# Zero rows under two matrix products, and a margin on the landings in a planned schedule

## The chip, the cores and the metric

One core of a Trainium2 chip runs the whole program. The time is the device time of one execution in microseconds, the median of the runs shown. The profile is of one execution of its own, so sums over its rows are set against that execution's time.

## The reference

The input x is 32 images of 96 channels and 56 x 56 pixels, float32. Two residual layers follow each other; each begins with a group normalisation over groups of three channels.

```python
x = x + _L0_conv_ref(_gn(x), ...)
x = x + _L1_conv_ref(_gn(x), ...)
```

Layer 0 is an inverted bottleneck with quantised weights and activations: a 1x1 convolution from 96 to 576 channels, batch norm, clipping to 4 bits; a 3x3 depthwise convolution, batch norm, clipping to 4 bits; a 1x1 convolution back to 96 channels, batch norm.

Layer 1 splits the 96 channels into three parts of 32. One goes through a gated 3x3 convolution, one through a fractional Fourier transform, a gated 1x1 mix, the inverse transform and an absolute value, and one through a real FFT, a gated 1x1 mix and the inverse FFT. The gates are small networks on channel means. The three parts are joined and go through a last 3x3 convolution from 96 to 96 channels.

## The kernel before

Each image is 96 partitions by 3136 floats and is worked on alone; images overlap only through the order of the instructions. Three buffers hold x.

Layer 0. `split` (line 702) normalises a quarter of the image (the four parities of row and column) into v on VectorE, rounds it on ScalarE to `hi`[...], and takes the rest `lo` on GpSimd. `expand` (712) multiplies both by w1 into a pair of PSUM banks: 2 halves by hi and lo, 392 columns each, with a contraction over 96 rows; this is tile pe. ScalarE's Relu (line 662) writes 8-bit levels q1s, VectorE masks them (666). Then the levels go to DRAM (sd, line 738) and come back in another layout (d, 746) for the depthwise products pd (756), which are column-tiled: 128 rows by 64 columns, two side by side. Their levels q2s go to DRAM (gd, 777) and come back (q, 780) for the projection pp (786), which adds into x (796). There are 5 blocks of 128 channels, the last of 64, so pe, pd and pp share two PSUM pairs in a fixed rotation.

Layer 1. `norm` (859) writes a part of F, which goes to DRAM (xd, 868) and back in another layout (xh, 875). Small products pf, pu, pi, pv carry out the transform forward and back. The result pq goes to DRAM (pd, line 1024, another tensor than the PSUM tile of that name) and comes back as F in four transfers (1029 and 1033, two each). `mix_f` (1041) multiplies F, 98 rows, by the gates into pz (line 1047), squares, adds, takes the root and copies into cat on GpSimd. `spatial` (1122, tile ps) and `mix_t` (1103, tile px) write the other parts of cat. `winograd` (1144) turns cat on VectorE into V, T and U, and `final` (1174) multiplies six slices V by the transformed weights wc into pc (line 1179): float32, 96 rows by 96 columns, 392 columns moving, three taps each. The results are added to x, and `store` writes x out.

The order has two makers. `arrange` (381) runs through three streams of steps, head (statistics and split), body (the rest of layer 0) and rest (layer 1), and picks the next step by how far each stream is through its work plus a lead in images: -0.8, 0.0 and 1.0 (line 1298). This fixes the order in which buffers and PSUM banks are handed round. Then the class `Order` plans every instruction: `model` (208) gives each a duration, and each DMA a time to landing (line 236); `pack` (277) is a list scheduler that puts them on the engines by rank[...]. `schedule` (339) tries 3 x 8 rankings and keeps the shortest plan. `hold` fixes each engine's order from it. A plan's times bind nothing on the chip; only its order does, and every engine takes its instructions in that order.

All DMAs of the steady state are issued by SyncE, in one order.

Of the kernel before, what the change touches and what calls it, by code (L numbers as in the profile page):

```python
# [52 lines left out]
F32 = mybir.dt.float32  # L53
# [25 lines left out]
BN_EPS = 1e-5  # L79
WINDOW, CHANGE = 3.4133, 0.09  # L80
TURNS, NEAR = 8, (2.0, 4.0, 8.0)
SLACK = 0.3


# [58 lines left out]
class Order:  # L143
# [64 lines left out]
    def model(self):  # L208
# [3 lines left out]
        for i, e, access in zip(self.ins, self.eng, self.access):  # L212
# [6 lines left out]
            if i.opcode == "DMACopy":  # L219
                took = 0.47 if e == "SP" else 0.4  # L220
                for a in (outs[0], ins[0]):
                    run = size = _bytes(a.dtype)
                    dims, n = list(a.ap), 1.0
                    if self.tiles.get(a.tensor.name, "dram") != "dram":
                        n = dims.pop(0)[1]
                        move = max(move, _count(a) * size / 7000.0 * min(n / 16.0, 1.0))
                    for _, c in dims:
                        n *= c
                    for step, c in reversed(dims):
                        if step * size == run or c == 1:  # L230
                            run *= c
                        else:
                            break
                    run = min(run, n * size / 16)
                    move = max(move, math.ceil(n * size / run / 16) * (0.011 + run / 21e3))
                lag = 1.6 + move + (0.3 if ins[0].tensor.name.startswith(("in_x", "sd", "gd")) else 0.0)
            elif e == "PE":
                cols, weights, rows = _count(ins[0]), _count(ins[1]), ins[0].ap[0][1]
                full = all(str(a.dtype) == "dt.float32" for a in ins)
                beside = weights in (G, 64) and cols >= HN  # L240
                if i.is_transpose:
                    took = max(cols / 1175.0, 0.055)
                    work = cols / 1200.0
                elif full:
                    took = 2 * max(cols / 1175.0, min(weights * 0.85e-3, 1.0), 0.05)
                    work = cols / 600.0
                else:
                    took = max(cols / (2180.0 if "float32r" in str(ins[1].dtype) else 2350.0), 0.05)
                    work = cols / 2400.0
                if beside and not i.is_transpose:  # L250
                    took, work = took * weights / 128.0, work * weights / 128.0
                kind = (0 if rows <= 32 else 1 if rows <= 64 else 2), weights if beside else 0
                work *= rows / 128.0
            elif e == "Activation":
                out = _count(outs[0])
                bias = sum(_count(a) == 1 for a in ins) > 1
                took = 0.1 + bias * 0.1 + out / 960.0 + (0.08 if out > 700 and psum[0] else 0.13 if out < 8 else 0.0)
            elif e == "DVE":
                port = n > 8 and not any(psum)
                if port and i.opcode == "TensorScalarPtr" and len(wide) == 1:  # L260
                    took = 0.15 + n / 1920.0 + (0.12 if n >= 700 else 0.0)
                else:
                    port = port and len(wide) > 1
                    took = (0.14 if n > 8 else 0.16) + n / 960.0 + (0.06 if any(psum) and "ScalarPtr" in i.opcode else 0.0)
            elif e == "Pool":
                port = True
                took = 0.1 + n * (2.25 if len(wide) > 1 else 1.1) / 1000.0 if n > 8 else 0.5
            else:
                took = 0.1
# [178 lines left out]
def block_kernel(ctx: ExitStack, tc: tile.TileContext, out: bass.AP, a: dict):  # L448
# [38 lines left out]
    with tc.tile_pool(name="prep", bufs=1) as pp:  # L487
# [22 lines left out]
                nc.vector.tensor_copy(dst, w, saturate=False)  # L510


        w1 = cp.tile([C, 128 * NB], F32R, tag="w1r", name="w1r")
        nc.vector.memset(w1[:, HID:].bitcast(F32), 0.0)
        quantise(load_tmp("w1"), C, "1", w1[:, :HID])
        w2 = load_tmp("w2")
        quantise(w2, 128, "2")
        nc.vector.tensor_tensor(w2, w2, load_tmp("mask2"), ALU.mult)
# [50 lines left out]


        raw = load_tmp("wc")
        wc = cp.tile([C, 6, 3 * C], F32, tag="wcw", name="wcw")
        tap = lambda k: raw[:, 3 * C * k : 3 * C * (k + 1)]
        sm = pp.tile([C, 3 * C], F32, tag="wsum", name="wsum")
        nc.vector.tensor_scalar(wc[:, 0, :], tap(0), 1.0 / 4, None, ALU.mult)
# [50 lines left out]
        q2.append(t)  # L626
    s0 = cp.tile([128, QS], F32, tag="s0", name="s0")
    nc.gpsimd.memset(s0, 0.0)
    cat = cp.tile([C, H + 2, W + 2], F32, tag="cat", name="cat")
    nc.gpsimd.memset(cat, 0.0)  # L630

    def group_stats(s, stats, name):

# [39 lines left out]
    def layer0(i):  # L673
# [16 lines left out]
        def norm():  # L690
            mean, rstd = s["mean"], s["rstd"]
            stats2[i] = p2.tile([C, 8, 6], F32, tag="bn2", name=f"bn2{i}")

            ab = p2.tile([C, 2], F32, tag="ab", name=f"ab{i}")
            nc.vector.tensor_scalar(ab[:, 0:1], rstd, 1.0, None, ALU.add)
            nc.vector.tensor_scalar(ab[:, 1:2], mean, rstd, None, ALU.mult)
            nc.vector.tensor_tensor(ab[:, 1:2], B3, ab[:, 1:2], ALU.subtract)
            s["ab"] = ab
            s["hi"] = p1.tile([C, 4, 2 * HN], F32R, tag="hi", name=f"hi{i}")
            s["lo"] = p1.tile([C, 4, 2 * HN], F32R, tag="lo", name=f"lo{i}")  # L700

        def split(u):
            v = p1.tile([C, 2 * HN], F32, tag="v", name=f"v{i}_{u}")
            nc.vector.tensor_scalar(  # L704
                v.rearrange("p (h w) -> p h w", w=HH), parity(u), s["mean"], s["rstd"], ALU.subtract, ALU.mult
            )
            nc.scalar.copy(s["hi"][:, u, :], v)  # L707
            nc.gpsimd.tensor_tensor(s["lo"][:, u, :], v, s["hi"][:, u, :].bitcast(F32), ALU.subtract)  # L708
            if u == 3:
                nc.gpsimd.tensor_scalar(xts[i], xts[i], s["ab"][:, 0:1], s["ab"][:, 1:2], ALU.mult, ALU.add)  # L710

        def expand(b, u):
            k = blk(b)
            ps = pair(f"pe{i}_{b}_{u}")
            for half in range(2):
                for n, part in enumerate((s["hi"], s["lo"])):
                    nc.tensor.matmul(  # L717
                        ps[:, half, :HN],
                        w1[:, 128 * b : 128 * (b + 1)],
# [134 lines left out]
    def layer1(i):  # L854
# [289 lines left out]
        def winograd(half, part):  # L1144
# [1 line left out]
            pitch = W + 2  # L1146
            n = 7 * pitch
            if part == 0:
                s["V", half] = p1.tile([C, 6, n], F32, tag=("torus", "F")[half], name=f"V{i}_{half}")
                s["T"] = p1.tile([C, 4, n], F32, tag="cs", name=f"T{i}_{half}")  # L1150
                s["U"] = p1.tile([C, 7, 2 * pitch], F32, tag="Z", name=f"U{i}_{half}")
            V, T, U = s["V", half], s["T"], s["U"]

            d = lambda j, m: view(catf, pitch * (28 * half + j), [[4 * pitch, 7], [1, m * pitch]])
# [19 lines left out]
        def final(half, k):  # L1174
# [3 lines left out]
            for dx in range(3):  # L1178
                nc.tensor.matmul(  # L1179
                    ps[:C, :HN],  # L1180
                    wc[:, k, C * dx : C * (dx + 1)],
                    V[:, :, dx : dx + W],
                    start=(dx == 0),
                    stop=(dx == 2),
                )
# [109 lines left out]
        rest += layer1(i)  # L1295
    for x in head[:13]:
        x.after.pop((-1, "e", NB - 1, 3), None)
    arrange([head, body, rest], loose, {"pair": 2, "bank": 4}, [-0.8, 0.0, 1.0], B)
    Order(nc.cur_bb.bb.instructions, tiles).hold(tc)


# [218 lines left out]
```

## Time and profile before

| what | value |
|---|---|
| median of three runs | 3350.51 us (3349.19 to 3354.25) |
| the profiled execution | 3364.8 us |
| its span, first to last instruction | 3363.0 us |
| mean granted TensorE clock | 0.949 |
| VectorE / ScalarE / GpSimd busy | 69% / 62% / 17% |
| DMA moved | 469.92 MB, 140 GB/s |
| waits of ScalarE for pd | 454.5 us |
| pe on hi and on lo | 1280 each, 416 and 344 ns |

In the rows of the profile a product is named by the PSUM tile it writes, then what it reads, then rows * columns of the array. A float32 product is two instructions, so pc has 2304 for 1152 products. The number in square brackets in a timeline is idle time of that engine just before, with what ended it.

### The profile page before, as it was taken

The numbers are of one execution on the slowest core, as the hardware profiler recorded it, in microseconds if no ns is written. First come the engines' busy times: TensorE is split into PE (matmuls) and PEld (weight loads), VectorE is DVE, ScalarE is ACT, GpSimd is POOL, SyncE is SP. The second block draws the span as 40 slices with busy tenths as digits, with TensorE's granted clock in tenths as the row PEclk, the third lists the DMA queues.
The fourth block names the chain that finished last, engine by engine and source line by source line (L and its number), as shares of the span: only waits on it lengthen the run. The fifth ranks groups of instructions, "written<-read, shape, count | busy, mean of one in ns | idle before, by whom it ended". The sixth has DMA issues, their size and how long they took to land. (4 is left out here: it accounts for less than half of the span.)

```text
span 3363.0 us, 47042 instructions
## 1 busy us (share of the span) xinstructions
PE 2961.3 (88%) x17024; PEld 1824.1 (54%) x17024; DVE 2331.5 (69%) x4497; ACT 2085.9 (62%) x2792; POOL 585.2 (17%) x657
## 2 busy tenths in 40 slices
PE   3789998889998889999899999898998898999987
PEld 2455565455565555555455565455565455565544
DVE  5357677677777676777677777676777676777755
ACT  3566665576666566656566666566666576666543
POOL 3122101222101222111222011222111222101100
PEclk9898999999999999999999999999999999999987
DMA  4545564455655455654455655455655455655432
GB/s 125 150 118 143 147 166 133 116 144 144 167 159 141 117 145 137 168 141 134 124 146 151 173 146 149 121 146 138 168 157 142 116 145 143 166 162 148 115 89 51
DMA packets 436800, 469.92 MB, mean 140 GB/s; under 512 B 203174, under 2 KB 351640, under 8 KB 435544
## 3 DMA queue, kind: packets, MB, share of 16 engines
q1 hardware_dynamic: 432384, 464.18, 51.6%
q10 hardware_dynamic: 4184, 2.74, 0.3%
q8 instruction: 135, 2.21, 0.3%
q14 instruction: 97, 0.79, 0.1%
HBM read 266.85 MB, written 199.97 MB: 139 GB/s over the span
## 5 line engine op out<-in xcount | busy, mean ns | idle before, releaser
L662 ACT ACTIVATE q2s<-pd,o,s 128x784 uint8<-128x784 f32 x576 | 558.3, 1002 | 473.9 <-PE pd L756 454.5
L1179 PE MATMUL pc<-V,wcw 96*96 96x392 f32 x2304 | 834.9, 502 | 18.1 <-DVE V L1164 18.1
L662 ACT ACTIVATE q1s<-pe,o,s 128x784 uint8<-128x784 f32 (+1 forms) x640 | 624.1, 1004 | 219.7 <-PE pe L717 213.5
L717 PE MATMUL pe<-hi,w1r 96*128 96x392 f32 x1280 | 532.7, 416 | 68.0 <-ACT q1s L662 32.1
L1179 PEld LDWEIGHTS pc<-V,wcw 96*96 96x96 f32 x2304 | 366.9, 164 | 338.9 <-issue 319.7
L756 PE MATMUL pd<-d,dw 128*64 128x392 fp8e4 x4608 | 471.1, 345 | 85.1 <-DMA d<-sd 78.2
L717 PE MATMUL pe<-lo,w1r 96*128 96x392 f32 x1280 | 440.6, 344 | 3.2 <-POOL lo L708 3.2
L756 PEld LDWEIGHTS <-dw 128*64 128x64 bf16 x4608 | 243.3, 113 | 297.8 <-DMA d<-sd 104.8
L717 PEld LDWEIGHTS pe<-hi,w1r 96*128 96x128 f32 x1280 | 242.9, 190 | 181.4 <-ACT q1s L662 88.2
L708 POOL TENSOR_TENSOR lo<-v,hi 96x784 fp32r<-96x784 f32 x128 | 243.4, 1901 | 287.9 <-ACT hi L707 274.6
L1047 PE MATMUL pz<-F,g 98*32 98x392 f32 x1024 | 178.0, 700 | 129.3 <-DMA F<-pd 79.3
L786 PE MATMUL pp<-q,w3q 128*96 128x392 fp8e4 x1280 | 269.5, 359 | 12.1 <-DMA q<-gd 9.5
L717 PEld LDWEIGHTS pe<-lo,w1r 96*128 96x128 f32 x1280 | 244.2, 191 | 27.5 <-POOL lo L708 4.2
L786 PEld LDWEIGHTS <-w3q 128*96 128x96 fp8e4 x1280 | 167.2, 135 | 154.4 <-issue 70.6
L666 DVE TENSOR_SCALAR q2s<-q2s 128x392 uint32<-128x392 uint32 x288 | 119.4, 421 | 182.9 <-ACT q2s L662 180.0
L796 DVE SCALAR_TENSOR_TENSOR x<-pp,s,x 96x392 f32<-96x392 f32 x256 | 146.1, 617 | 103.9 <-PE pp L786 103.7
L654 POOL TENSOR_TENSOR stb<-veb,mhalf 96x1 f32<-96x1 f32 x32 | 17.9, 561 | 1143.8 <-DVE veb L653 1143.8
L1060 POOL COPY cat<-sq 32x392 f32<-32x392 f32 x256 | 157.8, 616 | 295.7 <-ACT sq L1056 286.1
L666 DVE TENSOR_SCALAR q1s<-q1s 128x436 uint32<-128x436 uint32 (+1 forms) x320 | 122.6, 389 | 120.5 <-ACT q1s L662 99.6
L704 DVE TENSOR_SCALAR v<-x,sta 96x784 f32<-96x784 f32 x128 | 87.0, 680 | 161.1 <-POOL lo L708 139.5
L1126 PE MATMUL ps<-s,g 128*128 128x392 f32 x512 | 193.6, 503 | 0.0
L1140 ACT ACTIVATE cat<-ps,b 32x392 f32<-32x392 f32 x256 | 158.8, 620 | 46.2 <-PE ps L1126 42.5
(156 smaller groups left out, 4267.8 us busy)
## 6 DMA issues: line engine op xcount, KB each, us to landing
d<-sd SPq DMA_DIRECT2D x288, 435.5 KB
gd<-q2s SPq DMA_DIRECT2D x288, 196.0 KB
sd<-q1s SPq DMA_DIRECT2D x256, 218.0 KB
q<-gd SPq DMA_DIRECT2D x128, 392.0 KB
x<-in_x_dram SPq DMA_DIRECT2D x128, 294.0 KB
out_dram<-x SPq DMA_DIRECT2D x128, 294.0 KB
pd<-pq SPq DMA_DIRECT2D x32, 808.5 KB
F<-pd SPq DMA_DIRECT2D x64, 392.0 KB
```

The lines of the kernel that those rows point to most:

```text
L662: nc.scalar.activation(dst, ps, AF.Relu, bias=offset, scale=scale)
L666: nc.vector.tensor_scalar(w, w, 4, 0x0F0F0F0F, ALU.logical_shift_right, ALU.bitwise_and)
L708: nc.gpsimd.tensor_tensor(s["lo"][:, u, :], v, s["hi"][:, u, :].bitcast(F32), ALU.subtract)
L717: nc.tensor.matmul(ps[:, half, :HN], w1[:, 128 * b : 128 * (b + 1)], part[:, u, HN * half : HN * (half + 1)], start=(n == 0), stop=(n == 1),)
L756: nc.tensor.matmul(ps[64 * t : 64 * (t + 1), half, :HN], dw[n][:, 2 * t + y, :], view(s["d"][b, g][:, t, :], PQ * (14 * half + y), [[PQ, 1 ...
L786: nc.tensor.matmul(ps[:C, half, :HN], w3[:, b * C : (b + 1) * C], q2[b][:, u, HN * half : HN * (half + 1)], start=(b == 0), stop=(b == NB ...
L796: nc.vector.scalar_tensor_tensor(part, src, A3, part, ALU.mult, ALU.add)
L1047: nc.tensor.matmul(ps[G * j : G * (j + 1), :HN], s["g1"][: 3 * G + 2, G * q : G * (q + 1)], s["F"][:, 2 * HN * j + HN * h : 2 * HN * j + H ...
L1060: nc.gpsimd.tensor_copy(cat[G : 2 * G, r : r + 7, 1 : 1 + W], src)
L1126: nc.tensor.matmul(ps[:, :HN], s["g0"][:, 128 * t : 128 * (t + 1)], view(s0, PQ * (14 * half + t // 2) + t % 2, [[PQ, 14], [1, HH]]), star ...
L1140: nc.scalar.activation(dst, src, AF.Identity, bias=b0[2 * G : C], scale=1.0)
L1179: nc.tensor.matmul(ps[:C, :HN], wc[:, k, C * dx : C * (dx + 1)], V[:, :, dx : dx + W], start=(dx == 0), stop=(dx == 2),)
```

## The change

The products pe and pc contract over 128 rows in place of 96; the 32 rows added are zeros. For this w1 becomes a tile of 128 partitions, all set to zero before the weights are written into the first 96. hi and lo become one tile each for the whole kernel, with rows 96 to 127 set to zero once, in place of a new tile for each image. The weights wc lie in a tile wcz of 128 partitions with its last rows zero. cat, V, T and U get 128 partitions; cat's last rows stay zero from its first memset, and VectorE's operations that make V, T and U run over all 128 partitions.

The planner adds MARGIN, 0.8 us, to each DMA's time to landing. The lead of layer 1 in `arrange` goes from 1.0 to 0.95 images.

```diff
+MARGIN = 0.8
...
-                lag = 1.6 + move + (0.3 if ins[0].tensor.name.startswith(("in_x", "sd", "gd")) else 0.0)
+                lag = 1.6 + MARGIN + move + (0.3 if ins[0].tensor.name.startswith(("in_x", "sd", "gd")) else 0.0)
...
-        w1 = cp.tile([C, 128 * NB], F32R, tag="w1r", name="w1r")
-        nc.vector.memset(w1[:, HID:].bitcast(F32), 0.0)
-        quantise(load_tmp("w1"), C, "1", w1[:, :HID])
+        w1 = cp.tile([128, 128 * NB], F32R, tag="w1r", name="w1r")
+        nc.vector.memset(w1.bitcast(F32), 0.0)
+        quantise(load_tmp("w1"), C, "1", w1[:C, :HID])
...
-        wc = cp.tile([C, 6, 3 * C], F32, tag="wcw", name="wcw")
+        wcz = cp.tile([128, 6, 3 * C], F32, tag="wcw", name="wcw")
+        nc.gpsimd.memset(wcz[C:], 0.0)
+        wc = wcz[:C]
...
-    cat = cp.tile([C, H + 2, W + 2], F32, tag="cat", name="cat")
+    cat = cp.tile([128, H + 2, W + 2], F32, tag="cat", name="cat")
     nc.gpsimd.memset(cat, 0.0)
+    hi, lo = (cp.tile([128, 4, 2 * HN], F32R, tag=k, name=k) for k in ("hi", "lo"))
+    for t in (hi, lo):
+        nc.gpsimd.memset(t[C:].bitcast(F32), 0.0)
...
-            s["hi"] = p1.tile([C, 4, 2 * HN], F32R, tag="hi", name=f"hi{i}")
-            s["lo"] = p1.tile([C, 4, 2 * HN], F32R, tag="lo", name=f"lo{i}")
...
-            nc.scalar.copy(s["hi"][:, u, :], v)
-            nc.gpsimd.tensor_tensor(s["lo"][:, u, :], v, s["hi"][:, u, :].bitcast(F32), ALU.subtract)
+            nc.scalar.copy(hi[:C, u, :], v)
+            nc.gpsimd.tensor_tensor(lo[:C, u, :], v, hi[:C, u, :].bitcast(F32), ALU.subtract)
...
-                for n, part in enumerate((s["hi"], s["lo"])):
+                for n, part in enumerate((hi, lo)):
...
-                s["V", half] = p1.tile([C, 6, n], F32, tag=("torus", "F")[half], name=f"V{i}_{half}")
-                s["T"] = p1.tile([C, 4, n], F32, tag="cs", name=f"T{i}_{half}")
-                s["U"] = p1.tile([C, 7, 2 * pitch], F32, tag="Z", name=f"U{i}_{half}")
+                s["V", half] = p1.tile([128, 6, n], F32, tag=("torus", "F")[half], name=f"V{i}_{half}")
+                s["T"] = p1.tile([128, 4, n], F32, tag="cs", name=f"T{i}_{half}")
+                s["U"] = p1.tile([128, 7, 2 * pitch], F32, tag="Z", name=f"U{i}_{half}")
...
-                    wc[:, k, C * dx : C * (dx + 1)],
+                    wcz[:, k, C * dx : C * (dx + 1)],
...
-    arrange([head, body, rest], loose, {"pair": 2, "bank": 4}, [-0.8, 0.0, 1.0], B)
+    arrange([head, body, rest], loose, {"pair": 2, "bank": 4}, [-0.8, 0.0, 0.95], B)
```

## The prediction

> **What bounds the kernel now.** I read the page first (shares, clock row, costliest groups), then the waits, then one period of the steady state: TensorE's and SyncE's timelines and the busy time by stretches. The page says that TensorE is the engine to watch, and that its clock is not full.
>
> ```profile
> span 3363.0 us, 47042 instructions
> PE 2961.3 (88%) x17024; PEld 1824.1 (54%) x17024; DVE 2331.5 (69%) x4497; ACT 2085.9 (62%) x2792; POOL 585.2 (17%) x657
> PEclk9898999999999999999999999999999999999987
> L1179 PE MATMUL pc<-V,wcw 96*96 96x392 f32 x2304 | 834.9, 502 | 18.1 <-DVE V L1164 18.1
> L1047 PE MATMUL pz<-F,g 98*32 98x392 f32 x1024 | 178.0, 700 | 129.3 <-DMA F<-pd 79.3
> ```
>
> The reader is to see two things: 402 us (3363.0 less 2961.3) in which TensorE does nothing, and a granted clock of 0.949 on average. Nearly a third of that idle time, 129.3 us, stands before one small product, pz (line 1047). The timelines of TensorE and SyncE around one such place:
>
> ```profile
> 1010.73 1.55 PE L1110 MATMUL px<-torus,g 128*32 128x392 f32 x16
> 1012.07 0.26 PE L1112 MATMUL px<-pat,bias 128*32 128x56 f32 x2
> 1016.30 4.14 PE L1047 MATMUL pz<-F,g 98*32 98x392 f32 x20 [3.97 <-ACT cat L1120]
> 1020.37 2.81 PE L786 MATMUL pp<-q,w3q 128*96 128x392 fp8e4 x12
> ...
> 1003.40 0.32 SPq L1024 DMA_DIRECT2D pd<-pq  x1
> ...
> 1008.62 1.19 SPq L1029 DMA_DIRECT2D F<-pd  x2
> 1009.86 2.13 SPq L1033 DMA_DIRECT2D F<-pd  x1
> 1012.03 0.53 SPq L777 DMA_DIRECT2D gd<-q2s  x1
> 1012.60 0.78 SPq L1033 DMA_DIRECT2D F<-pd  x1
> ```
>
> The wait is put down to ScalarE's copy of cat, but that copy starts at 1015.73 and frees nothing that pz reads; what pz reads is F, whose fourth transfer is issued only at 1012.60. One image later the same wait (3.81 us before 1116.14) is put down to F<-pd. In TensorE's timeline 28 of the 32 images have this gap before pz, 3.6 to 6.0 us, 123 us in all. A second gap, before pd (line 756) and put down to d<-sd, is there in 9 images: 33 us.
>
> Behind each gap the clock is halved. [...]the columns are busy us of TensorE, weight loads, VectorE, ScalarE, GpSimd (instructions in brackets), the clock, DMA share and GB/s:
>
> ```profile
> 1011.39:1014.81 3.42, 0.94 (x14) 0.37 (x9) 1.00 (x2) 3.33 (x7) 1.84 (x1) 1.00 1.34 160
> 1014.81:1018.22 3.41, 1.92 (x12) 0.69 (x16) 2.33 (x5) 2.01 (x5) 1.85 (x1) 0.50 0.35 93
> 1018.22:1021.63 3.41, 3.41 (x16) 1.28 (x9) 2.04 (x2) 2.76 (x4) 3.17 (x2) 0.50 0.01 3
> 1021.63:1025.04 3.41, 3.41 (x24) 1.67 (x23) 2.41 (x5) 0.53 (x1) 3.26 (x4) 1.00 0.00 0
> ...
> 100.06:103.46 3.40, 1.52 (x16) 0.81 (x16) 0.36 (x1) 2.80 (x4) 0.00 (x0) 1.00 0.80 217
> 103.47:106.87 3.40, 0.00 (x0) 0.00 (x0) 0.86 (x2) 0.96 (x2) 1.83 (x1) 1.00 0.40 61
> ...
> 632.54:635.95 3.41, 1.95 (x9) 1.32 (x8) 1.42 (x4) 3.41 (x5) 1.55 (x3) 1.00 0.24 77
> 635.95:639.36 3.41, 0.38 (x4) 0.23 (x6) 2.97 (x4) 0.08 (x1) 2.24 (x2) 0.50 0.68 192
> ```
>
> In all, 338 us run at half clock, about 100 windows in some 48 episodes (0.051 of the clock lost, times two, times the span).[...] The window from 100.06 holds 16 pd products of 128 rows[...] and the next stays fast. The one from 632.54 holds [...]pe products with 96 rows, and the next is slow.[...]
>
> [...]the 128-row ps (line 1126) takes 503 ns, the 96-row pc 502, both f32 with 392 columns.[...]
>
> **The change, part by part.**
>
> *Zero rows.* pe (lines 717) and pc go from 96 to 128 rows: by the rows above 0 ns an instruction, 4864 of them.[...] Gain 10 us. The pz episodes don't change by this: their windows are filled with pz, which keeps 98 rows, and pp, which has 128.[...]
>
> *VectorE on 128 partitions.* The V, T, U operations do the same number of elements a partition (T 1867 ns for 1624): nothing.
>
> *Memsets at the start.* w1: 640 columns in place of 64 (0.11 us); a 576-column pass takes 1.04 us (line 505), so 1.2 at most, and VectorE idles from 0.9 to 10.2 us. hi and lo: two of 3136, like cat's 3364 in 3.17 us, so 2 x 2.95; wcw's rows 1728, 1.6. GpSimd idles 7.6 us before sta and 9.6 before the first lo, which hides 7.5 us. Nothing; uncovered, 7.5 us once.
>
> *hi and lo kept for good.* An image's first split no longer waits for all readers of the tile before, only for those of its own quarter. In the stretch above the splits of the next image run from 1005 to 1018, while the last pe of this one ended at 984: they wait for x and its statistics, not for the tile. Nothing.
>
> *The margin.* It changes no instruction, only the planner's idea of when data is there, so the order. Two hops lead to pz. The planner prices pd at 0.47 + 1.6 + 7 x (0.011 + 7392/21000) = 4.6 us; in the timeline F's first issue follows pd's by 5.2. It prices F's four at 0.47 + 0.63 + 2 x 2.43 + 2 x 0.09 + 0.97 = 7.1 us; pz starts 7.7 after the first issue. Together it is 1.2 us short, and the margin gives 1.6. SyncE alone explains part: a line-1033 issue takes 2.0 us (median), the planner says 0.47. The other 2.8 of the usual 4.4 us are not a mispriced landing: they are either in the plan or come from elsewhere, and the margin won't fill them. What could fill even the 1.6? pp waits for the last block's q (issued 1016.00), its two open sums hold both PSUM pairs, so pe of the next image can't start; pc waits for pz. Work must be moved here from the pd, pp and ps of the 10 us before, which leaves a smaller gap there. So I take half.
> In full: 28 x 1.6 = 45 us idle[...]. The pd gap: 9 x 1.6 = 14[...]. Sum 80, half is 40 us. Bounds: 0 and 80.
> A margin adds no wait. But consumers are put later: behind a pz put later stand sq, cat, V and pc, and behind pc the store and the load of x three images on.
>
> *Lead 1.0 to 0.95.* Layer 1 is taken 0.05 image, 5 us of the 101 us between one pz and the next 20 times over, earlier against layer 0. It fixes which PSUM bank follows which; its sign I can't read. Zero, with 60 us either way.
>
> Sum: 10 + 40 = 50 us off the profiled execution's 3364.8, so 3315. The median of the runs shown, 3350.5, lies 14.3 below that execution; there it is 3300.
>
> **Rivals.**
>
> *The gap is filled.* Lead and margin together move F's wait under the depthwise products. For it: 1035 to 1085 us TensorE is idle for 0.4 us, so work abounds one stage away. Against it: what blocks here is PSUM and q. Then all of 123 + 63 goes at best, say three quarters, and 10 of padding: 3350 - 150 = 3200.
>
> *The plan already holds the wait.* Then the margin only names it, and padding alone pays: 3340. For it: 2.8 of 4.4 us have no mispriced hop. Against it: the planner ranks by the whole chain and shifts whole groups.
>
> *Longer plan, slower kernel.* x has three buffers: load, statistics, split, layer 0, layer 1 and store of one image make a loop of three periods. Ten DMA hops lie on it (x; sd, d, gd, q of the last block; xd, xh, pd, F; out): 10 x 0.8 / 3 = 2.7 us a period in the plan, 85 us over 32. If half of that becomes real, since consumers that used to start at once now stand behind other work in TensorE's queue, it is 40 us more than before: 3390. For it: x is loaded at 985, right behind the store of 975 to 980. Against it: at most hops data does come later than planned. It decides from where the distance from pz to pz passes 102 us.
>
> **How the numbers follow.** Partly filled, 0.52: 3300, own range 3265 to 3335. Filled, 0.15: 3200. Padding alone, 0.13: 3340, half of it within 0.2% (7 us, about what a measurement of this kernel can tell from no change). Slower, 0.20: 3390, of which 0.01 within. Faster 0.74, same 0.07, slower 0.19. The range, 3200 to 3372, leaves out half of each outer case.
>
> **What would show it.** Right: the gap before pz falls from 4.4 to about 2.8 us or less, half-clock windows from 100 to about 75, clock about 0.96, pe and pc as long as before, hops as long as before. Wrong: pz's gap unchanged in most images (padding alone); gaps of over 3 us before pe, pp or pf that weren't there (longer plan); pe or pc over 1% longer each (rows are not free).

## The result: no change, and where the idle time went

The changed kernel takes 3351.39 us (median of 12 runs, 3339.75 to 3367.20) against 3355.18 for the kernel before in the same session. The ratio of the mean times is 1.0001, with a 95% interval of [0.9984, 1.0018] (the ratio of the two medians is 0.9989). The forecast was 3300. Its profiled execution took 3365.41 us (before 3364.8).

The page of the changed kernel: span, busy time of each engine, granted clock in 40 slices, the row of pc.

```profile
span 3363.6 us, 47169 instructions
PE 2972.1 (88%) x17024; PEld 1832.9 (54%) x17024; DVE 2340.7 (70%) x4497; ACT 2091.1 (62%) x2792; POOL 626.0 (19%) x660
PEclk9889999999999999999999999999999999999997
L1184 PE MATMUL pc<-V,wcw 128*96 128x392 f32 x2304 | 835.7, 499 | 13.0 <-DVE V L1169 13.0
```

TensorE is idle for 391.5 us (3363.6 less 2972.1), it was 401.7. Half-clock time is 319 us, it was 343 (the prediction's 338 is a slip: its own product gives 343), and the mean clock 0.953 instead of 0.949. The zero rows cost no time: pc is 499 ns for 502, pe on lo 349 for 344, and from the start of one pc instruction to the next the median is 329 ns in both. (Lines have shifted by 5 to 7.) So nearly all idle time is still there. It isn't where it was. These are groups by line, first of the kernel before, then of the changed kernel, with the idle time just before each in the last column (pz of the kernel before stands in the prediction):

```profile
L756 PE MATMUL pd<-d,dw 128*64 128x392 fp8e4 x4608 | 471.1, 345 | 85.1 <-DMA d<-sd 78.2 <-ACT q2s L662 5.2 <-ACT q1s L662 1.2
L786 PE MATMUL pp<-q,w3q 128*96 128x392 fp8e4 x1280 | 269.5, 359 | 12.1 <-DMA q<-gd 9.5 <-ACT q2s L662 2.1 <-DVE x L796 0.5
L986 PE MATMUL pu<-u,e2t 112*114 112x456 f32 x128 | 63.9, 604 | 10.7 <-ACT u L977 10.6
...
L761 PE MATMUL pd<-d,dw 128*64 128x392 fp8e4 x4608 | 470.3, 345 | 29.7 <-DMA d<-sd 21.6 <-ACT q1s L669 5.0 <-ACT q2s L669 2.2
L791 PE MATMUL pp<-q,w3q 128*96 128x392 fp8e4 x1280 | 277.5, 375 | 86.2 <-DVE x L801 73.0 <-DMA q<-gd 11.3 <-ACT q2s L669 1.7
L1052 PE MATMUL pz<-F,g 98*32 98x392 f32 x1024 | 134.8, 595 | 78.1 <-DMA F<-pd 59.4 <-DVE cat L1123 13.5 <-DVE v L709 5.1
L991 PE MATMUL pu<-u,e2t 112*114 112x456 f32 x128 | 81.0, 746 | 71.8 <-ACT u L982 71.7
```

Before pz the idle time fell from 129.3 to 78.1 us, before pd from 85.1 to 29.7: 107 us less, where the prediction asked 59 us of the margin (45 and 14, before it halved the sum). But before pp it rose from 12.1 to 86.2 and before pu from 10.7 to 71.8: 135 us more. The margin isn't the only cause of this move. Every edit here, the zero rows too, makes the planner choose another order, and in the run with the zero rows alone (e1 below) pz and pu stand much as they do in the changed kernel:

```profile
L1052 PE MATMUL pz<-F,g 98*32 98x392 f32 x1024 | 143.1, 631 | 76.4 <-DMA F<-pd 75.3 <-DVE cat L1123 0.7 <-issue 0.3
L991 PE MATMUL pu<-u,e2t 112*114 112x456 f32 x128 | 74.9, 672 | 73.3 <-ACT u L982 70.2 <-ACT torus L1093 2.5 <-DVE torus L1091 0.3
```

The prediction had held that the waits before pz don't change by the zero rows. One place in TensorE's timeline of the changed kernel:

```profile
1014.77 1.20 PE L791 MATMUL pp<-q,w3q 128*96 128x392 fp8e4 x6
1018.16 4.63 PE L1052 MATMUL pz<-F,g 98*32 98x392 f32 x32 [2.19 <-DMA F<-pd]
1022.72 2.52 PE L791 MATMUL pp<-q,w3q 128*96 128x392 fp8e4 x14
1026.82 3.35 PE L791 MATMUL pp<-q,w3q 128*96 128x392 fp8e4 x19 [1.58 <-DVE x L801]
```

and VectorE's timeline beside it:

```profile
1021.07 0.68 DVE L709 TENSOR_SCALAR v<-x,sta 96x784 f32<-96x784 f32 x1 [0.86 <-POOL lo L713]
1021.67 0.56 DVE L1060 TENSOR_TENSOR sq<-sq 128x392 f32<-128x392 f32 x1
1024.62 0.95 DVE L709 TENSOR_SCALAR v<-x,sta 96x784 f32<-96x784 f32 x1 [2.40 <-POOL lo L713]
1025.61 2.22 DVE L801 SCALAR_TENSOR_TENSOR x<-pp,s,x 96x392 f32<-96x392 f32 x4
```

Projection products now stand ahead of pz, so its wait is 2.19 us here, where the same place before had 3.97. But pp needs a PSUM bank back, which VectorE's add into x (line 801) gives; that add stands in VectorE's queue behind v (line 709) of the next image, and v waits 2.40 us for GpSimd's lo. A new wait, with the same work behind it.

### The profile page after: what moved, and what is told of

The parts are those of the page before. It is cut to its first block, busy times and chain, and to the rows that moved or that the text cites. A ratio compares the mean times of both kernels' runs of the same rounds, so it can differ in the third digit from the quotient of the medians.

```text
span 3363.6 us, 47169 instructions
## 1 busy us (share of the span) xinstructions
PE 2972.1 (88%) x17024; PEld 1832.9 (54%) x17024; DVE 2340.7 (70%) x4497; ACT 2091.1 (62%) x2792; POOL 626.0 (19%) x660
## 5 line engine op out<-in xcount | busy, mean ns | idle before, releaser
L1184 PE MATMUL pc<-V,wcw 128*96 128x392 f32 x2304 | 835.7, 499 | 13.0 <-DVE V L1169 13.0
L722 PE MATMUL pe<-hi,w1r 128*128 128x392 f32 x1280 | 519.5, 406 | 50.2 <-DVE x L801 21.2
L1184 PEld LDWEIGHTS pc<-V,wcw 128*96 128x96 f32 x2304 | 363.6, 163 | 315.6 <-issue 298.2
L761 PE MATMUL pd<-d,dw 128*64 128x392 fp8e4 x4608 | 470.3, 345 | 29.7 <-DMA d<-sd 21.6
L722 PE MATMUL pe<-lo,w1r 128*128 128x392 f32 x1280 | 444.8, 349 | 3.2 <-POOL lo L713 3.2
L791 PE MATMUL pp<-q,w3q 128*96 128x392 fp8e4 x1280 | 277.5, 375 | 86.2 <-DVE x L801 73.0
L722 PEld LDWEIGHTS pe<-hi,w1r 128*128 128x128 f32 x1280 | 243.8, 191 | 167.3 <-ACT q1s L669 75.6
L722 PEld LDWEIGHTS pe<-lo,w1r 128*128 128x128 f32 x1280 | 245.3, 192 | 22.8 <-POOL lo L713 4.2
L661 POOL TENSOR_TENSOR stb<-veb,mhalf 96x1 f32<-96x1 f32 x32 | 30.3, 947 | 1135.3 <-DVE veb L660 1135.3
L1052 PE MATMUL pz<-F,g 98*32 98x392 f32 x1024 | 134.8, 595 | 78.1 <-DMA F<-pd 59.4
L1145 ACT ACTIVATE cat<-ps,b 32x392 f32<-32x392 f32 x256 | 158.4, 619 | 41.2 <-PE ps L1131 37.2
L1007 PEld LDWEIGHTS pi<-e,cs 114*114 114x114 f32 x1088 | 133.8, 189 | 58.6 <-issue 52.1
L673 DVE TENSOR_SCALAR q2s<-q2s 128x392 uint32<-128x392 uint32 x288 | 103.9, 361 | 87.2 <-ACT q2s L669 87.0
```

What stands on the lines that cost most here:

```text
L673: nc.vector.tensor_scalar(w, w, 4, 0x0F0F0F0F, ALU.logical_shift_right, ALU.bitwise_and)
L722: nc.tensor.matmul(ps[:, half, :HN], w1[:, 128 * b : 128 * (b + 1)], part[:, u, HN * half : HN * (half + 1)], start=(n == 0), stop=(n == 1),)
L761: nc.tensor.matmul(ps[64 * t : 64 * (t + 1), half, :HN], dw[n][:, 2 * t + y, :], view(s["d"][b, g][:, t, :], PQ * (14 * half + y), [[PQ, 1 ...
L791: nc.tensor.matmul(ps[:C, half, :HN], w3[:, b * C : (b + 1) * C], q2[b][:, u, HN * half : HN * (half + 1)], start=(b == 0), stop=(b == NB ...
L1052: nc.tensor.matmul(ps[G * j : G * (j + 1), :HN], s["g1"][: 3 * G + 2, G * q : G * (q + 1)], s["F"][:, 2 * HN * j + HN * h : 2 * HN * j + H ...
L1145: nc.scalar.activation(dst, src, AF.Identity, bias=b0[2 * G : C], scale=1.0)
```

## The experiments

"Period" is the mean distance from the first pz of one image to that of the next, over images 4 to 28, from each run's trace; it was 100.80 us before and is 100.57 after. Ratios are to the kernel before on the same chip, with 95% intervals. Three theories come up: P, that TensorE's gaps are lost time and the margin moves or fills them; L, that the loop of the three x buffers sets the period; and R, the ring, that layer 1 of one image can't begin before that of the image before has ended, so that its whole chain is one period long. A caution for all of them: nearly every edit leads the planner to another order of the instructions, so a run shows its edit together with that order. Only e9 has the order of the kernel that it is set against.

**The parts and their pairs.** e1: zero rows alone. e2: margin alone. e3: lead alone. e5: zero rows and margin. e6: zero rows and lead.

```diff
 e1, from after     -MARGIN = 0.8                +MARGIN = 0.0
                    -[-0.8, 0.0, 0.95]           +[-0.8, 0.0, 1.0]
 e2, from before    -lag = 1.6 + move            +lag = 1.6 + 0.8 + move
 e3, from before    -[-0.8, 0.0, 1.0]            +[-0.8, 0.0, 0.95]
 e5, from after     -[-0.8, 0.0, 0.95]           +[-0.8, 0.0, 1.0]
 e6, from after     -MARGIN = 0.8                +MARGIN = 0.0
```

> Zero rows and the kept hi and lo alone; no margin, lead 1.0. Theory A (waits only move: the stretch where both layers wait has a fixed length, whatever the order): 0.996 to 1.004 of before, with the gap before pz still about 4.4 us in most images. Theory B (the parts have real effects of opposite sign that cancel): padding saves the 10 us that I had priced, 0.995 to 0.998, with fewer half-clock windows before pd.

> The margin of 0.8 us alone; no zero rows, lead 1.0. Theory A: 0.997 to 1.004; the gap before pz falls to about 2 us, and new gaps of the same sum stand before pp, pu or pe. Theory B: clearly off 1, either 0.985 to 0.99 (margin good, lead bad) or 1.01 and more (margin bad, the others good).

> The lead of 0.95 alone; no zero rows, no margin. Theory A: 0.997 to 1.004. Theory B: clearly off 1 by 0.5% or more, with the sign opposite to the margin's.

> The changed kernel with the lead back at 1.0: zero rows and margin. If the margin's loss of 1.3% (seen alone) is its own: 1.008 to 1.012 of before, with the gap before pd in most images as with the margin alone. If it came from one unlucky phase of the two layers that the lead mends: the same, so this can't tell these two apart, but a result at 1.000 would say that the zero rows change the plan enough to undo it.

> The changed kernel with MARGIN 0: zero rows and lead 0.95. If the parts add: 0.9965 x 1.0022 = 0.9987 of before, so that the margin inside the change would cost 0.14%. If the margin helps once the lead is right: 1.003 or more.

| lead | zero rows | no margin | margin |
|---|---|---|---|
| 1.0 | no | 1 | e2: 1.0126 [1.0109, 1.0143] |
| 1.0 | yes | e1: 0.9965 [0.9954, 0.9975] | e5: 1.0098 [1.0079, 1.0117] |
| 0.95 | no | e3: 1.0022 [1.0003, 1.0041] | e9 (below): 1.0026 [1.0010, 1.0041] |
| 0.95 | yes | e6: 0.9990 [0.9978, 1.0003] | the change: 1.0001 [0.9984, 1.0018] |

Down each column the zero rows take 0.25 to 0.35% off. The margin costs 1.3% at lead 1.0; at 0.95 it is 0.1%, within the noise. The lead costs 0.2% without a margin and gains 1.0% with it. So the change is a gain of 0.3% by the zero rows and a loss of about as much by margin and lead together. That the two cancel to 1.0001 is chance. Of the theories A and B in these expectations, A falls with e2. B is right about the zero rows and the margin, but not about the lead, whose sign alone isn't opposite to the margin's. In e5 the time is what was expected, but its idle time stands before pc (162.2 us) and not before pd.

In e2 the margin does to pz what it was to do. Two groups of e2, then two lines of TensorE's timeline:

```profile
L756 PE MATMUL pd<-d,dw 128*64 128x392 fp8e4 x4608 | 488.2, 355 | 156.3 <-DMA d<-sd 139.0 <-ACT q2s L662 13.1 <-ACT u L977 2.1
L1047 PE MATMUL pz<-F,g 98*32 98x392 f32 x1024 | 120.4, 514 | 12.1 <-DMA F<-pd 9.3 <-ACT cat L1120 2.8
```

```profile
1028.28 2.82 PE L756 MATMUL pd<-d,dw 128*64 128x392 fp8e4 x16 [3.99 <-DMA d<-sd]
1032.81 3.58 PE L1179 MATMUL pc<-V,wcw 96*96 96x392 f32 x5 [1.71 <-DVE V L1164]
```

The wait before pz is gone (12.1 us for 129.3). Products pe of the next image fill its place, and with them used up, pd waits for its data some 4 us in 31 places: 156.3 us for 85.1. Here this gap and the next, before pc, are 3 us apart and stand at half clock together (0.50 in each stretch from 1025.90 to 1036.10). TensorE's idle time in all is 423 us, for 402 before, half-clock time 424 us for 343, and the clock 0.938. So the wait was filled, and TensorE was idle for longer.

**Rows, with the order held.** e9 has the instructions of the changed kernel in its order on every engine, with only the rows of pe and pc back at 96; its planner is told that they have 128.

```diff
-                        w1[:, 128 * b : 128 * (b + 1)],
-                        part[:, u, HN * half : HN * (half + 1)],
+                        w1[:C, 128 * b : 128 * (b + 1)],
+                        part[:C, u, HN * half : HN * (half + 1)],
...
-                    wcz[:, k, C * dx : C * (dx + 1)],
-                    V[:, :, dx : dx + W],
+                    wcz[:C, k, C * dx : C * (dx + 1)],
+                    V[:C, :, dx : dx + W],
```

> The changed kernel with pe and pc contracting over 96 rows again; the planner still counts 128 rows for them, so every engine's order is that of the changed kernel. It isolates what the zero rows do on the chip. If rows weigh[...]: slower than the changed kernel by 5 to 20 us, some more windows at half clock, and pe and pc no shorter. If rows don't weigh: the same time and the same number of windows at half clock as the changed kernel.

1.0026 [1.0010, 1.0041], against 1.0001 of the changed kernel. The groups of e9:

```profile
L1187 PE MATMUL pc<-V,wcw 96*96 96x392 f32 x2304 | 842.9, 502 | 12.6 <-DVE V L1172 12.6
L725 PE MATMUL pe<-hi,w1r 96*128 96x392 f32 x1280 | 524.8, 410 | 53.8 <-DVE x L804 25.5 <-ACT hi L715 15.0 <-ACT q1s L672 9.2
```

Its products are as long (pc 502 ns) and its half-clock time is 340 us instead of 319. Over all runs its mean clock is 0.951 (16 runs), that of the changed kernel 0.956 (12 runs). With the same order on every engine, that is what the rows did to the granted clock. In time it is 0.25%, and the two ratios' intervals overlap. The four pairs of the table have one sign, but in three of them the order differs too.

**What sets the period.** e12: the changed kernel with three x tiles for good, so that each quarter of x can be loaded as soon as it is free. e13: the kernel before with two x buffers in place of three (a load then waits for the store two images back). e18: the kernel before with the operation `norm` (line 863) done three times over. e14: e1 with pz over 128 rows, the rows added to F being zeroed by GpSimd for each image.

```diff
 e12 -        xt = xp.tile([C, HW], F32, tag="x", name=f"x{i}")
     +        xt = xbuf[i % 3]
 e13 -tc.tile_pool(name="xp", bufs=3)), "xp", 3, tiles)
     +tc.tile_pool(name="xp", bufs=2)), "xp", 2, tiles)
 e18 +            for _ in range(3):
                      nc.vector.tensor_scalar(s["F"][2 * G : 3 * G], ...)
 e14 -            s["F"] = p1.tile([G * 3 + 2, HW], F32, tag="F", name=f"F{i}")
     +            s["F"] = p1.tile([128, HW], F32, tag="F", name=f"F{i}")
     +            nc.gpsimd.memset(s["F"][3 * G :], 0.0)
     -                        s["g1"][: 3 * G + 2, G * q : G * (q + 1)],
     +                        s["g1"][:, G * q : G * (q + 1)],
```

> The changed kernel with three x tiles kept for good, so that a quarter of x is loaded as soon as that quarter of the image three before is stored, not when all of it is. This shortens the loop load, layer 0, layer 1, store by some 3 to 5 us. If that loop of three periods holds the period (theory L): a third of it a period, 1.0 to 1.7 us, 32 to 54 us in all, 0.984 to 0.990 of the changed kernel. If not: within 0.4% of the changed kernel.

> The kernel before with two buffers of x in place of three. It measures the loop itself: with two, a period is at least half of one image's way from load to store. Theory L (the loop is tight with three): that way is about 300 us even with less company on the engines, so some 150 us a period and 4600 us or more. If the way is much shorter than 300 us when it isn't held up by other work, say 240: 120 us a period, about 3850 us, and the loop isn't what sets 101 us with three.

> The kernel before with layer 1's first operation on F (line 863, 1.9 us on VectorE) done three times over, with the same result; 3.8 us more between one image's last pc and the next image's xd. Theory R (layer 1 is a ring of one period: F takes the place of the V that the last pc of the image before reads, so norm, xd, xh, pf, pu, pi, pv, pd, F, pz, cat, winograd, pc run one after the other and their length is the period): 3.8 us a period, 31 times, 118 us, 1.03 to 1.036 of before. Theory L (the ring of three periods over the x buffers): a third, 1.010 to 1.013. Theory P (TensorE's sum of work and waits): within 0.4%.

> Zero rows alone (no margin, lead 1.0), and pz too: F gets 128 rows, its last 32 set to zero by GpSimd for each image before the two single rows land.[...] If rows weigh: 15 to 25 windows at half clock fewer than with zero rows under pe and pc alone; under theory R only what stands in the ring counts, pz itself, 1 to 2 us a period at best: 0.985 to 0.997 of before.

L has no support. e12 is slower, 1.0187 [1.0163, 1.0211], which neither reading of it had. e13 takes 4182 us with a period of 128.2 us, between its two readings. With two buffers an image goes through in two periods, 256 us, less than the 302 that three periods give now; so the way of an image can be shorter than the three buffers allow.

The ring has support. e18: 1.0490 [1.0461, 1.0520], where P had no change and R 1.030 to 1.036. VectorE's timeline there, the three passes of `norm`:

```profile
1649.12 1.90 DVE L864 TENSOR_SCALAR F<-x,stb 32x3136 f32<-32x3136 f32 x1
...
1652.41 1.90 DVE L864 TENSOR_SCALAR F<-x,stb 32x3136 f32<-32x3136 f32 x1
...
1654.76 1.90 DVE L864 TENSOR_SCALAR F<-x,stb 32x3136 f32<-32x3136 f32 x1
```

The third ends 5.6 us after the first. From the last pc of an image to the next xd it takes 9.0 us in the mean, 3.9 before, and the period grows from 100.80 to 105.92: 5.1 us in both. TensorE is idle for 432 us there, and VectorE is busy 70% of the time. The match is partly luck: the order differs, other stretches of the chain moved by up to 5 us, and half-clock time rose from 343 to 490 us, in which products take about twice as long (in before pp follows pp after 166 ns at full clock and 327 at half, pc follows pc after 329 and 654). Why the chain is closed is seen around the last product of an image, first in the kernel before, then in e1:

```profile
1176.47 0.55 POOL L654 TENSOR_TENSOR stb<-veb,mhalf 96x1 f32<-96x1 f32 x1 [35.78 <-DVE veb L653]
1177.42 1.48 PE L1179 MATMUL pc<-V,wcw 96*96 96x392 f32 x4
1177.57 1.90 DVE L881 TENSOR_SCALAR torus<-x,stb 32x3136 f32<-32x3136 f32 x1
1179.80 0.55 DVE L1220 TENSOR_TENSOR x<-x,pc 96x392 f32<-96x392 f32 x1
1180.39 1.90 DVE L863 TENSOR_SCALAR F<-x,stb 32x3136 f32<-32x3136 f32 x1
...
1063.16 0.90 PE L1184 MATMUL pc<-V,wcw 128*96 128x392 f32 x2
1065.36 1.90 DVE L868 TENSOR_SCALAR F<-x,stb 32x3136 f32<-32x3136 f32 x1
1067.29 0.31 SPq L873 DMA_DIRECT2D xd<-F  x1
```

F and half of V share a buffer (tag "F" in the diff). So `norm` of the next image can begin only when the last pc has read V. It starts 1.98 us after the start of the last pc in every image of before, 0.53 in after, 1.12 in e2, to within 0.01 us over 24 images. In after it waits for that pc itself. In before and e2 it stands in VectorE's queue behind the addition of pc to x. A second limit is as near: the statistics of the next image (the first line above, stb) are ready only 1.9 us before the last pc ends. From `norm` on, xd, xh, pf, pu, pi, pv, pd, F, pz, cat, V and pc follow each other to the next last pc.

e14 lengthens the ring in the same place: 1.0318 [1.0297, 1.0338], where a small gain was expected. Its operations on F (minimum, median and maximum in ns):

```profile
L1053 PE MATMUL pz<-F,g x1024: 488/517/863, 211.8 to 3423.4; 128*32 128x392 f32 x171
L868 POOL MEMSET F<- x32: 2706/2806/3517, 45.9 to 3375.4; 32x3136 f32 x32
L869 DVE TENSOR_SCALAR F<-x,stb x32: 1902/1904/3785, 143.0 to 3378.7; 32x3136 f32<-32x3136 f32 x32
```

The memset of 2.8 us comes ahead of `norm`, which starts 3.5 us later after the last pc than in e1 (medians, 4.83 for 1.36), and the period is 3.8 us longer. The shorter time at half clock that was expected did not come (356 us, 299 in e1).

**The ring cut in one place.** In e16, from e1, xd no longer comes from F: VectorE writes the values into spare partitions of the x tile, right after the second part of the statistics, and F gets its copy later. These two parts of the statistics and the new operation also move from layer 1's stream of steps to the end of layer 0's. e17 is the changed kernel with the same edit; e20 is e16 with lead 0.95, e21 is e16 with the margin, e19 is e17 with pz over 128 rows as in e14.

```diff
-        xt = xp.tile([C, HW], F32, tag="x", name=f"x{i}")
+        xt = xp.tile([128, HW], F32, tag="x", name=f"x{i}")
-        xts[i] = xt
+        xts[i], tails[i] = xt[:C], xt[C:]
+        def early():
+            mean, rstd = s["mean"], s["rstd"]
+            nc.vector.tensor_scalar(tails[i], xts[i][G : 2 * G], mean[G : 2 * G], rstd[G : 2 * G], ALU.subtract, ALU.mult)
...
-            nc.sync.dma_start(out=s["xd"], in_=s["F"][2 * G : 3 * G])
+            nc.sync.dma_start(out=s["xd"], in_=tails[i])
...
-        body += b
-        rest += layer1(i)
+        r = layer1(i)
+        body += b + r[:3]
+        rest += r[3:]
```

> Zero rows alone (no margin, lead 1.0), and the ring of layer 1 cut open: the normalised part that goes to DRAM is written to rows 96 to 127 of the x tile, which no other image shares, right after the statistics, which now stand at the end of layer 0's stream; F gets its own copy later, 1.9 us more of VectorE an image. Theory R: norm, xd and xh, some 12 us, leave the ring, so the period falls until something else holds it, 3% at least, 0.93 to 0.966 of before. Theories L and P: 0.992 to 1.003.

> The same cut in the changed kernel (zero rows, margin, lead 0.95). Theory R: 0.93 to 0.97 of before; and with the ring open the margin may be worth something, so that it could come out ahead of the same cut without a margin. Theories L and P: 0.995 to 1.006.

> The changed kernel, its ring cut (e17, 0.983), and pz over 128 rows as in e14. In e14 GpSimd's memset of F stood in the ring before norm (norm began 4.8 us after the last pc, not 1.4) and cost 3.5%. Theory R: with norm out of the ring the memset costs little, and pz at full clock is a gain of up to 1 us a period: 0.975 to 0.985. If the loss in e14 came from something else[...]: 1.01 or more.

> Zero rows, the ring cut (e16), and the lead of 0.95; no margin. With the ring cut, zero rows alone stood at 0.990 and margin and lead together at 0.983. If the lead brings the difference: 0.983. If the margin brings it: 0.990. If each needs the other, as with the ring closed: 0.990 to 0.995.

> Zero rows, the ring cut (e16), and the margin of 0.8 us; lead 1.0. If the margin's loss of 1.3% came only through the ring (its consumers put later lengthen the ring): with the ring cut it is no loss, 0.983 to 0.991. If it is a loss of its own: 1.000 or more.

| run | margin | lead | ratio | period, us |
|---|---|---|---|---|
| e16 | no | 1.0 | 0.9902 [0.9881, 0.9924] | 98.72 |
| e20 | no | 0.95 | 0.9893 [0.9870, 0.9916] | 99.54 |
| e21 | yes | 1.0 | 1.0197 [1.0166, 1.0228] | 102.80 |
| e17 | yes | 0.95 | 0.9832 [0.9815, 0.9848] | 98.68 |

The cut is worth 0.6% on e1 and 1.7% on the changed kernel, and e17, at 3299.04 us, is the fastest kernel of the study. R had expected 3% at least, so it missed too. In e16 the cut did not bring xd forward: it starts 5.7 us after the start of the last pc in the mean, later than in e1 (3.4), so the 0.6% can't be put down to a shorter way to xd. What holds it are the statistics. An image of e16, lines of VectorE, TensorE and SyncE in order of time:

```profile
1049.62 0.37 DVE L648 BATCH_NORM_AGGREGATE mvb<-bn 96x2 f32<-96x48 f32 x1
1060.99 0.25 PE L650 MATMUL pmb<-mvb,gmat 96*96 96x1 f32 x2
1061.10 2.20 PE L1188 MATMUL pc<-V,wcw 128*96 128x392 f32 x6
1063.13 0.25 PE L658 MATMUL pvb<-gtb,gmat 96*96 96x1 f32 x2
1064.62 1.90 DVE L890 TENSOR_SCALAR torus<-x,stb 32x3136 f32<-32x3136 f32 x1
1066.56 1.91 DVE L873 TENSOR_SCALAR x<-x,stb 32x3136 f32<-32x3136 f32 x1
1068.49 0.33 SPq L877 DMA_DIRECT2D xd<-x  x1
```

Their sums (mvb) are there 11 us earlier, but the two small products pmb and pvb stand among the last products pc in TensorE's order, as they do in before, and the operation `torus` stands ahead of the new one. Why the planner puts them there wasn't taken apart. In e17 they stand earlier, and xd starts 0.9 us before the last pc instead of 2.5 after it as in the changed kernel; the period is 1.9 us shorter there. Its half-clock time is also the lowest of all runs, 172 us, and the two can't be told apart. In e17 and e16 VectorE has 1.9 us more to do for each image, off the ring, and the time falls; so it isn't VectorE's work as such that made e18 longer.

The margin behaves here as it did before: bad at lead 1.0 (3.0% over e16, where the expectation had it harmless once the ring is cut), good at 0.95 (0.6% under e20). e19 has 1.0051 [1.0039, 1.0062], 2.2% over e17 and outside both of its readings. A likely reason: GpSimd's memset of F stands in its queue waiting for the buffer, the longest of these waits 34.2 us (total, times and longest in this line of the waits):

```profile
POOL F L868 <- PE pc L1189: 128.5, 29, 34.2
```

**Which landings cost the margin.** e22 is e1 with the margin on xd, xh, pd and F alone, the ring's own hops; e23 is e1 with it on all the others; e24 is e16 with it on the ring's hops.

```diff
 e22, e24  +lag = 1.6 + MARGIN * outs[0].tensor.name.startswith(("xd", "xh", "pd", "F")) + move + ...
 e23       +lag = 1.6 + MARGIN * (not outs[0].tensor.name.startswith(("xd", "xh", "pd", "F"))) + move + ...
```

> Zero rows, lead 1.0, the margin of 0.8 us on four landings only: xd, xh, pd and F, the hops of layer 1's own ring. If the loss of the margin (e2 1.013, e5 1.010, against 0.9965 for the zero rows alone) comes from these hops, whose consumers on TensorE are put behind other work: 1.008 to 1.012 of the time before, with pf and pz starting over 1 us later after their data than in e1. If it comes from the other hops (d, q, x, the stores): 0.995 to 0.999. If both this run and its complement lose, or neither does: the plan as a whole decides, and no hop carries it.

> The complement of e22: zero rows, lead 1.0, the margin on every landing but xd, xh, pd and F. If the ring's hops carry the loss: 0.995 to 0.999 of the time before. If the others do (d, q, x, the stores): 1.008 to 1.012, with the wait before pd or pp longer than in e1.

> e16 (zero rows, lead 1.0, ring cut before xd) with the margin on xd, xh, pd and F only. If a margin on these four hops is worth 1.2% by itself, as e22 against e1, it is worth that here too: 0.976 to 0.982 of the time before, with the gaps before pz and pu gone. If what a margin brings is a matter of which plan it happens to lead to, the sum doesn't hold: above 0.985, and e22's gain is not to be carried over.

e22: 0.9849 [0.9806, 0.9892], against both readings. e23: 1.0014 [0.9997, 1.0031]. Against e1's 0.9965 the ring's margins gain 1.2%, the others lose 0.5%, and both together (e5) lose 1.3%. e24: 1.0113 [1.0087, 1.0139]; there the same four margins lose 2.1%. Groups of e22:

```profile
L761 PE MATMUL pd<-d,dw 128*64 128x392 fp8e4 x4608 | 476.6, 340 | 78.9 <-ACT q1s L669 54.2 <-DMA d<-sd 20.7 <-ACT q2s L669 3.3
L791 PE MATMUL pp<-q,w3q 128*96 128x392 fp8e4 x1280 | 258.8, 353 | 130.7 <-DMA q<-gd 116.1 <-DVE x L801 12.7 <-ACT q2s L669 1.7
L1052 PE MATMUL pz<-F,g 98*32 98x392 f32 x1024 | 146.4, 702 | 13.6 <-DMA F<-pd 8.3 <-ACT hi L712 5.3
```

and of e24:

```profile
L761 PE MATMUL pd<-d,dw 128*64 128x392 fp8e4 x4608 | 509.2, 364 | 128.3 <-DMA d<-sd 108.3 <-ACT q2s L669 16.7 <-ACT q1s L669 2.1
L1056 PE MATMUL pz<-F,g 98*32 98x392 f32 x1024 | 157.8, 560 | 6.1 <-DMA F<-pd 6.1
```

In both the wait before pz is gone, and in both another of some 110 us stands elsewhere. One kernel is 1.5% faster than before, the other 1.1% slower. TensorE's gaps don't tell which: those over 1.5 us sum to 280 us in before, 302 in after, 265 in e2, 265 in e22, 256 in e24. The next table shows where the period goes: the stretches of the ring, each from the first instruction named to the second (means in us over images 5 to 28, from the starts in each trace), and the half-clock time of the whole run. The sum is the distance from last pc to last pc, so it is the period whatever holds it; the table tells where the time lies and doesn't prove the ring.

| stretch | before | after | e1 | e2 | e22 | e24 |
|---|---|---|---|---|---|---|
| last pc to pf (norm, xd, xh) | 14.2 | 12.8 | 14.7 | 14.3 | 14.1 | 14.8 |
| pf to the last pv | 14.0 | 15.5 | 19.1 | 16.2 | 16.1 | 15.8 |
| to the first load of F | 6.8 | 6.4 | 5.7 | 6.8 | 6.3 | 6.0 |
| to the first pz | 7.9 | 8.4 | 7.8 | 9.3 | 9.4 | 9.4 |
| to the last pz | 9.5 | 4.1 | 5.0 | 6.1 | 6.6 | 12.6 |
| to the last copy into cat | 8.1 | 9.9 | 10.7 | 10.3 | 8.8 | 5.7 |
| to the first pc | 3.2 | 6.2 | 4.5 | 2.7 | 3.0 | 3.7 |
| to the last pc | 36.7 | 37.2 | 32.5 | 36.4 | 34.5 | 34.1 |
| sum | 100.5 | 100.6 | 100.0 | 102.3 | 98.8 | 102.0 |
| half-clock time of the run | 343 | 319 | 299 | 424 | 275 | 371 |

Read the fourth row first. Wherever the margin is on F at lead 1.0, F's first load to pz takes 9.3 or 9.4 us instead of 7.8 (9.6 in e5, 10.2 in e21): the plan has put work of layer 0 ahead of pz, and this stretch is 1.5 us longer or more. That is the price of a filled gap. The row above it is no shorter in e2 than in before, 6.8 us: F did not come earlier. The other rows move by up to 8 us either way (pz to last pz, 4.1 to 12.6), according to what the plan put between these steps, and they decide the sum: e22 pays the same price as e24 and is the faster by 2.6%.

Two things keep the ring from being the whole account. From the first pc to the last, TensorE is all but never idle (0.1 us of 37.2 in before), and a third of its work there is not pc but pe and pd of the next image, 6.5 and 5.7 us. Over this third of the ring TensorE itself is the bound, and a filled gap would pay if the work that fills it came from there. And the half-clock time in the last row goes nearly in the order of the sums. In the kernel before the clock falls to 0.50 at the end of a gap of over 3 us or within 2 us behind it at all 29 of them before pz and at 7 of 9 before pd (the prediction has it behind each), and in after at all 3 before pz and all 3 before pd; at half clock the products also take twice as long (the 327 ns for 166 of pp above). So this may be cause and effect at once. With the order held, 21 us of half-clock time (e9 against the change) went with 8 us of time. At that price, an estimate from these two profiled executions, the 96 us between e22 and e24 would be worth some 37 of the 90 us between them. No run parts the rest.

## Why the prediction was wrong

- **What bounds the kernel: wrong, and the rest follows from it.** The prediction took TensorE, idle 402 us, and priced each us of gap as a us of time. In e2 the largest gap is closed, and the kernel is 1.3% slower. What the runs support in its place is a chain of one period from `norm` to the last pc: in e18 5.1 us more from the last pc to xd go with 5.1 us more a period, in e14 3.5 us before `norm` with 3.8. That every step named lies on it, and nothing else, isn't shown: the cut of e16 and e17 gained 0.6 and 1.7% and not 3%, because the statistics hold almost as late. Two things in the profile of before could have shown the chain: `norm` starts 1.98 us after the last pc of the image before in each image, and F and V share a tag. That shared buffer isn't the whole of it either: in e16, where xd no longer comes from F, xd came no earlier.
- **The margin, the term of 40 us: the step that failed.** It was "Sum 80, half is 40 us. Bounds: 0 and 80." Of the 80, 59 us are idle time; the other 21, and the 63 us beside 123 in the first rival, are time lost to the clock, which the author estimated and no run shows. Alone it costs 1.26%, some 42 us. Up to the gap the mechanism was right: in e2, which has the margin alone, the wait before pz is gone, 117 us for the 45 asked. (In the change it is 2.2 us at the place shown, but the zero rows' order accounts for much of that, as e1 shows.) The next step, from gap to time, failed. The prediction did say that the work moved in leaves a smaller gap elsewhere, and took half for it. Measured, the gaps elsewhere took more than all: for those 117 us in e2, TensorE's idle time rose by 22 us in all and its half-clock time by 81. Nor did F come earlier; pz was put later behind other work. The bound of 0 was wrong too: the text itself names sq, cat, V and pc "behind a pz put later" and priced them at nothing.
- **The lead, "Zero, with 60 us either way".** 0.2% alone, 7 us. With the margin it takes 1.0%, some 33 us, off. The range was right; that it isn't a term of its own but hangs on the margin was not said.
- **Zero rows, 10 us: right in size.** The 10 us were the author's estimate; by what rule rows bear on the clock isn't shown. With the order held it is 0.25%, 8 us, with less half-clock time (319 us for 340) and no time an instruction (pc 499 ns for 502), as forecast. In e1 it is 0.35% (12 us), but there the order changed, and with it the waits before pz, which the prediction had left as they were.
- **VectorE on 128 partitions, memsets at the start: right.** The operation T takes 1870 ns for 1867. The first pz stands at 207.0 us after, 206.2 before. Hi and lo kept for good wasn't tried by itself.
- **The rivals.** "Longer plan, slower kernel" is what the margin does alone: 3397.7 us for the 3390 named, a period of 102.3 for the 102 from which it was to decide. Its reason, ten hops over three periods of the x loop, has no support in e12 and e13; that consumers stand behind other work in TensorE's queue is what e2 shows, on a chain of one period. "Padding alone", 3340, fits e1 in time, 3344.56, but not in mechanism: the margin doesn't only name a wait that the plan holds, it changes the time by itself.
- **The signs to look for.** The pz gap fell as told. The time at half clock fell only from 343 to 319 us, by 7%, where a quarter of the windows was to go, and the clock reached 0.953, not 0.96; over all 12 runs it is 0.956. The sign of the longer plan, gaps of over 3 us before pp, came in the change, which isn't slower (11 of them, 2 before), and not in e2, which is (1): there they stand before pd. So that sign doesn't tell a longer period.

What stays open: what fixes the length of the other stretches under one plan or another. The margin's effect ranged from -1.2% (e22 on e1) to +3.0% (e21 on e16), and the two sets of landings tried gave a gain and a small loss apart and a larger loss together. The margin on the ring's four hops changes its sign from e1 to e16. So e22's gain is shown for that kernel only. Open too is how much of each difference is the clock's.

## What to carry to other kernels

An engine's idle time before an operation is a gain only if that engine is the bound there: look first for a chain that closes on itself within one period, such as two tiles that share a buffer. Test it by making one step on it longer and seeing whether the period grows by as much, best with the order of everything else held, and then see what else becomes ready at the same place before cutting it. An edit to a planner's prices changes the whole order; forecast it as a spread (here from -1.2 to +3.0%), not as the gap it is aimed at, and measure each part with the others on and off. Rows of zeros that fill a contraction from 96 to 128 rows cost no time in the products here (pc 499 ns for 502) and lifted the mean clock from 0.951 to 0.956, with the order held, when they were written once; zeroing them again for each tile cost 3.5% (e14 against e1) where the memset stood on the chain.

## What the runs showed of the hardware

- With the order the same on every engine, 96 rows for 128 in pe and pc (e9 against the change) gave 340 us at half clock for 319 in the profiled executions, and a mean clock of 0.951 for 0.956 over all runs, at nearly equal lengths of the products (pc 502 ns for 499).
- The changed kernel's runs scatter more, 3339.75 to 3367.20 in 12 runs, than those of the kernel before beside them, 3348.86 to 3359.89; the scatter goes with the granted clock: it is 0.953 in the slowest of these runs and 0.959 in the fastest.
- Starved of x (e13), the kernel spends 1210 of 4180 us at half clock, and its mean clock is 0.856 (before 0.949). The same 17024 matrix instructions keep TensorE busy for 3329.4 us there and for 2961.3 before.
